# Group statistics of a normalisation: from averaging matmuls to transfers and VectorE sums

## Chip, cores, metric

The kernel runs on one core of one Trainium2 chip. The metric is the time of one execution in microseconds (us), lower is better. Several executions were timed for every kernel; all that are compared here ran fast, at a granted TensorE clock that averages 0.99 to 1.00 of full speed over the execution.

## The reference, cut to what matters

The input is 8 images of 64 channels and 64x64 pixels. Two layers follow each other, both with an attention over the 4096 pixels of an image. Only layer 1 normalises by groups of channels:

```python
# layer 0: attention with 8-channel keys and queries, plus its input
x = _L0_conv_ref(x, Wf, bf, Wg, bg, Wh, bh)

# layer 1: 8 groups of 8 channels
xg  = x.reshape(b, 8, 8, h, w)
mu  = mean(xg, axis=(2, 3, 4))
var = mean((xg - mu) ** 2, axis=(2, 3, 4))
xn  = (xg - mu) * rsqrt(var + 1e-5) * gamma + beta
q, k, v = split(w_qkv @ xn)                  # 64 channels each
x = w_proj @ (softmax(q k^T / 8) v) + x
```

## The kernel before

The 128 partitions hold the 64 channels twice, one half of the image in each. VectorE collects per-channel moments while layer 0 writes its result. Layer 1 of image b then needs, on each partition, the mean and the variance of the channel's group, which is spread over 16 partitions, 8 in each half. The kernel before fetched them across partitions with two matmuls against an averaging matrix, each of one column:

```python
gavg = const.tile([P, 2, GROUPS, GS], F32, name="gavg")     # 1/16 within a group, else 0
nc.gpsimd.memset(gavg, 0.5 / GS)
# ... eight affine_select on GpSimd cut it to blocks ...

def channels():
    vector.bn_aggr(mv, self.st())                 # mean and variance of each row

def means():
    ps = pair()                                   # borrows two PSUM banks
    matmul(ps[:, 0, 0:1], gavg, mv[:, 0:1], start=True, stop=True)
    nc.scalar.copy(mu, ps[:, 0, 0:1])
    vector.tensor_sub(d, mv[:, 0:1], mu)
    vector.scalar_tensor_tensor(v, d, d, mv[:, 1:2], op0=ALU.mult, op1=ALU.add)

def deviations():
    ps = pair()
    matmul(ps[:, 0, 0:1], gavg, v, start=True, stop=True)
    nc.scalar.copy(ve, ps[:, 0, 0:1])
    vector.tensor_scalar_add(ve, ve, EPS)
    # ... 1/sqrt(ve) by four Newton steps on VectorE, times gamma ...

at = [18, 22, 26] if self.b == 0 else [16, 20, 24]
units = [(at[0], channels, False), (at[1], means, True), (at[2], deviations, True)]
# ... then, from step 27 (b == 0) or 26 on: normal(c), project(c), values(c)
```

The numbers in `at` are steps of the attention that runs meanwhile. One step is one block of scores, their exponentials on ScalarE, their sum on VectorE, and the weighted sum of an earlier block on TensorE. `True` means that the unit borrows a pair of the eight PSUM banks. In a layer-0 stage TensorE makes scores in groups that fill the free banks, so a loan makes one group smaller and shifts all later groups. The order of TensorE's matmuls is fixed in the program; VectorE's is fixed too until the first layer-1 stage begins.

## Time and profile before

| | before |
|---|---|
| time, median of 3 | 3051.95 us (3050.56 to 3053.05) |
| span of the profiled run | 3050.3 us |
| layer 0 of images 0 and 1 (here "the opening") | up to 335.93 us |
| first layer-1 stage | 335.93 to 566.91, 230.98 us |
| each other layer-1 stage but the last two | 230.98 or 230.99 us |
| each layer-0 stage between them | 144.64 to 144.67 us |

### The profile page before, as it was taken

How to read it: one execution, taken by the hardware profiler on the slowest of the kernel's cores; microseconds unless marked ns; L12 is line 12 of the kernel's file. 1: busy time of each engine (PE TensorE's matmuls, PEld its weight loads, DVE VectorE, ACT ScalarE, POOL GpSimd, SP SyncE). 2: the span in 40 equal slices, each digit the busy share in tenths (PEclk: the TensorE clock that was granted, in tenths of full speed). 3: DMA queues.
4: the chain of work that ended last, by engine and by line, in shares of the span. 5: the costliest groups of instructions: out<-in, count | busy, mean ns of one | idle time of the engine just before them, and what ended most of it. 6: DMA issues, size and time to landing. Idle time of an engine off the chain costs nothing.

```text
span 3050.3 us, 58859 instructions
## 1 busy us (share of the span) xinstructions
PE 3023.2 (99%) x25857; PEld 1287.4 (42%) x25857; DVE 2596.0 (85%) x1668; ACT 2036.3 (67%) x1972; POOL 16.7 (1%) x45
## 2 busy tenths in 40 slices
PE   8999999999999999999999999999999999999998
PEld 3333335433354333533345333453334533345555
DVE  6999987899778998789987899779997799877776
ACT  6878655786557865578655785558855588555554
POOL 2000000000000000000000000000000000000000
PEclk9999999999999999999999999999999999999999
DMA  3000010100101001010010100100001000000000
GB/s 79 22 8 11 19 40 16 32 1 15 40 19 29 1 15 40 22 25 1 16 40 23 25 1 15 43 22 22 1 22 40 19 8 1 16 22 16 9 15 13
DMA packets 69816, 62.89 MB, mean 21 GB/s; under 512 B 43104, under 2 KB 43152, under 8 KB 69552
## 3 DMA queue, kind: packets, MB, share of 16 engines
q1 hardware_dynamic: 68560, 58.90, 8.0%
q8 instruction: 204, 3.34, 0.5%
q14 instruction: 60, 0.49, 0.1%
q0 software_dynamic: 672, 0.12, 0.0%
q10 hardware_dynamic: 320, 0.04, 0.0%
HBM read 25.06 MB, written 8.65 MB: 11 GB/s over the span
## 4 chain that ended last, share of the span: by engine, by line
PE 95%; DVE 3%; issue 1%; ACT 1%; DMA 0%; SPq 0%; DVEq 0%; ACTq 0%
PE banks L150 95%; DVE esum_l L140 3%; ACT e_l L917 1%; DMA x<-in_x_dram 0%; ACT full_l L542 0%; DVE rt L140 0%; DVE w_l L140 0%; DVE x L140 0%; SPq L179 0%; DVE raw_l L140 0%; DVE st_l L140 0%; DVE raw_end L140 0%; DVE guess_l L140 0%; DVE xn_l L140 0%; DVEq L140 0%
## 5 line engine op out<-in xcount | busy, mean ns | idle before, releaser
L140 DVE TENSOR_TENSOR esum_l<-esum_l,e_l 128x2048 f32<-128x2048 f32 x895 | 2048.7, 2289 | 363.5 <-ACT e_l L876 313.5
L876 ACT ACTIVATE e_l<-banks 128x1024 f32<-128x1024 f32 x1024 | 992.7, 1021 | 782.8 <-PE banks L150 761.0
L150 PE MATMUL banks<-e_l,v_l 64*64 64x512 f32 (+2 forms) x8772 | 1118.2, 588 | 0.0
L917 ACT ACTIVATE e_l<-banks 128x512 f32<-128x512 f32 (+3 forms) x767 | 956.9, 1311 | 194.0 <-PE banks L150 178.1
L150 PE MATMUL banks<-kq_l 64*64 64x512 f32 (+1 forms) x8448 | 1028.3, 586 | 3.4 <-ACT e_l L917 3.2
L150 PE MATMUL banks<-e_l,vt_l 128*64 128x512 f32 (+1 forms) x4060 | 832.1, 550 | 0.0
L150 PEld LDWEIGHTS banks<-e_l,v_l 64*64 64x64 f32 (+1 forms) x8772 | 439.7, 134 | 505.0 <-issue 466.8
L150 PEld LDWEIGHTS banks<-kq_l 64*64 64x64 f32 (+1 forms) x8448 | 422.9, 135 | 503.8 <-issue 468.3
L150 PEld LDWEIGHTS banks<-e_l,vt_l 128*64 128x64 f32 x4060 | 267.1, 137 | 471.3 <-issue 451.2
L150 PE MATMUL banks<-fg_l 32*128 32x512 f32 x1792 | 210.8, 460 | 6.4 <-ACT e_l L917 4.1
L150 PEld LDWEIGHTS banks<-fg_l 32*128 32x128 f32 x1792 | 85.9, 183 | 189.9 <-ACT e_l L917 139.1
L140 DVE TENSOR_TENSOR esum_l<-e_l,e_l 128x2048 f32<-128x2048 f32 x64 | 146.4, 2287 | 7.1 <-ACT e_l L876 7.1
L140 DVE TENSOR_TENSOR esum_l<-esum_l 128x1024 f32<-128x1024 f32 x63 | 76.9, 1221 | 0.9
L140 DVE TRANSPOSE_TENSOR_REDUCE part_l<-esum_l 128x32 f32<-128x1024 f32 x32 | 63.1, 1973 | 0.0
L140 DVE COPY raw_l<-banks 128x512 f32<-128x512 f32 x31 | 21.4, 692 | 30.6 <-PE banks L150 30.6
L140 DVE TENSOR_TENSOR raw_l<-raw_l,r_l 128x512 f32<-128x512 f32 x63 | 43.2, 685 | 0.0
L669 ACT ACTIVATE kq_l<-banks,qkb 128x512 f32<-128x512 f32 x64 | 40.6, 696 | 0.0
L150 PE MATMUL banks<-xn_l,wqk 64*64 64x512 f32 x256 | 35.5, 592 | 0.0
L150 PEld LDWEIGHTS banks<-wh,x 64*64 64x64 f32 x1024 | 25.3, 139 | 13.3 <-issue 12.4
L150 PEld LDWEIGHTS banks<-wvp,xn_l 64*64 64x64 f32 x1024 | 24.0, 134 | 13.0 <-issue 13.0
L577 ACT COPY raw_l<-banks 128x512 f32<-128x512 f32 x32 | 19.1, 596 | 11.6 <-PE banks L150 11.4
L140 DVE SCALAR_TENSOR_TENSOR x<-raw_l,hb,x 128x512 f32<-128x512 f32 x32 | 24.1, 752 | 1.1
(111 smaller groups left out, 404.4 us busy)
## 6 DMA issues: line engine op xcount, KB each, us to landing
r_l<-recips SPq DMA_DIRECT2D x126, 128.0 KB, 2.9
fg_l<-high_l SPq DMA_DIRECT2D x216, 64.0 KB, 2.0
kq_l<-kq_l SPq DMA_DIRECT2D x64, 128.0 KB, 2.3
out_dram<-raw_l SPq DMA_DIRECT2D x62, 128.0 KB, 2.4
x<-in_x_dram SPq DMA_DIRECT2D x30, 256.0 KB, 4.9
kq_l<-high_l SPq DMA_DIRECT2D x32, 64.0 KB, 2.0
part_l<-part_l SPq DMA_DIRECT2D x128, 4.0 KB, 1.8
zt_l<-zs_l SPq DMA_DIRECT2D x124, 1.0 KB, 1.7
```

The costliest lines, as they stand in the source:

```text
L140: it = getattr(nc.vector, name)(*args, **kwargs)
L150: in_order(nc.tensor.matmul(*args, **kwargs))
L577: nc.scalar.copy(raw, acc[0])
L669: nc.scalar.activation(self.parts[:, h, cols], ps[:, h, :], AF.Identity, bias=k1["qkb"][:, h : h + 1],)
L876: nc.scalar.activation(e[:, p], both_ps[p], AF.Exp, scale=at.scale)
L917: nc.scalar.activation(e.rearrange("k p h n -> k (p h) n")[:, first_ : first_ + n_, :], banks[:, bank : bank + n_, :], AF.Exp, scale=at.scale,
```

## The change

The intent: no matmul for the statistics. The mean and variance of each of the 128 rows (128x2 numbers, both halves of the image) go out to memory in one transfer and come back in four, laid out so that each partition has the 16 values of its group in its own row. VectorE sums them there. The units that read them are tied behind a sum of the steps before, so that the scheduler does not place them before the transfers have landed. The diff, with the removal of the averaging matrix and the move of a helper cut:

```diff
+    moments = [dram.tile([P, 2], F32, name=f"moments_{b}") for b in range(B)]
...
             def channels():
                 vector.bn_aggr(mv, self.st())
+                sent = moments[self.b]
+                nc.sync.dma_start(sent, mv)
+                for s in range(2):
+                    rows = sent[ts(s, C), :].rearrange("(g k) i -> g (k i)", k=GS)
+                    for h in range(2):
+                        nc.sync.dma_start(
+                            group[ts(h, C), s, :, :],
+                            rows.unsqueeze(1).broadcast_to([GROUPS, GS, 2 * GS]),
+                        )

             def means():
-                ps = pair()
-                matmul(ps[:, 0, 0:1], gavg, mv[:, 0:1], start=True, stop=True)
-                nc.scalar.copy(mu, ps[:, 0, 0:1])
-                vector.tensor_sub(d, mv[:, 0:1], mu)
-                vector.scalar_tensor_tensor(v, d, d, mv[:, 1:2], op0=ALU.mult, op1=ALU.add)
+                vector.tensor_reduce(mu, mean, axis=AX.X, op=ALU.add)
+                vector.tensor_scalar(mu, mu, 0.5 / GS, None, op0=ALU.mult)
+                vector.tensor_scalar(d, mean, mu, None, op0=ALU.subtract)
+                vector.tensor_mul(d, d, d)
+                vector.tensor_add(d, d, var)
+                vector.tensor_reduce(ve, d, axis=AX.X, op=ALU.add)

             def deviations():
-                ps = pair()
-                matmul(ps[:, 0, 0:1], gavg, v, start=True, stop=True)
-                nc.scalar.copy(ve, ps[:, 0, 0:1])
-                vector.tensor_scalar_add(ve, ve, EPS)
+                vector.tensor_scalar(ve, ve, 0.5 / GS, EPS, op0=ALU.mult, op1=ALU.add)
...
-            at = [18, 22, 26] if self.b == 0 else [16, 20, 24]
-            units = [(at[0], channels, False), (at[1], means, True), (at[2], deviations, True)]
+            at = [18, 23, 26] if self.b == 0 else [16, 22, 24]
+            units = [
+                (at[0], channels, False),
+                (at[1], behind(means), False),
+                (at[2], behind(deviations), False),
+            ]
```

`group` is a new tile of 128x32; `mean` and `var` are its two halves, and `d` becomes a tile of 16 columns.

More of the change, by code (lines that the diff above doesn't have):

```diff
@@ L122, in fast_path @@
     made_last = {}
+    added = None
     tight = False
@@ L150, in matmul, with behind, made @@
         in_order(nc.tensor.matmul(*args, **kwargs))
+    def behind(work_):
+        def made():
+            with tc.issue_after(added):
+                work_()
+        return made
     x_tiles = {}
@@ L229, in fast_path @@
     nc.vector.memset(ones, 1.0)
-    gavg = const.tile([P, 2, GROUPS, GS], F32, name="gavg")
-    nc.gpsimd.memset(gavg, 0.5 / GS)
-    for h in range(2):
-        for half in range(2):
-            rows = gavg[ts(half, C), h, :, :]
-            nc.gpsimd.affine_select(
-                out=rows, in_=rows, compare_op=ALU.is_ge, fill=0.0,
-                base=0, pattern=[[-GS, GROUPS], [0, GS]], channel_multiplier=1,
-            )
-            nc.gpsimd.affine_select(
-                out=rows, in_=rows, compare_op=ALU.is_ge, fill=0.0,
-                base=GS - 1, pattern=[[GS, GROUPS], [0, GS]], channel_multiplier=-1,
-            )
-    gavg = gavg.rearrange("p h g s -> p (h g s)")
     QP = 2 * CW // P
     stash = const.tile([P, (2 * B * NC - 1) * QP], F32, name="stash")
+    moments = [dram.tile([P, 2], F32, name=f"moments_{b}") for b in range(B)]
     recips = [dram.tile([P, QP], F32, name=f"recips_{i}") for i in range(2 * B * NC)]
@@ L597, in before @@
             mu = small.tile([P, 1], F32, tag="mu", name=f"mu_{n}")
-            v = small.tile([P, 1], F32, tag="v", name=f"v_{n}")
+            ve = small.tile([P, 1], F32, tag="ve", name=f"ve_{n}")
             self.mu, self.a = mu, small.tile([P, 1], F32, tag="a", name=f"a_{n}")
+            group = small.tile([P, 2, GS, 2], F32, tag="group", bufs=1, name=f"group_{n}")
+            mean, var = (group[:, :, :, i].rearrange("p s k -> p (s k)") for i in range(2))
+            d = small.tile([P, 2 * GS], F32, tag="d", bufs=1, name=f"d_{n}")
             def channels():
                 vector.bn_aggr(mv, self.st())
-            def means():
-                ps = pair()
-                matmul(ps[:, 0, 0:1], gavg, mv[:, 0:1], start=True, stop=True)
-                nc.scalar.copy(mu, ps[:, 0, 0:1])
-                d = small.tile([P, 1], F32, tag="d", name=f"d_{n}")
-                vector.tensor_sub(d, mv[:, 0:1], mu)
-                vector.scalar_tensor_tensor(v, d, d, mv[:, 1:2], op0=ALU.mult, op1=ALU.add)
-            def deviations():
-                ps = pair()
-                matmul(ps[:, 0, 0:1], gavg, v, start=True, stop=True)
-                ve = small.tile([P, 1], F32, tag="ve", name=f"ve_{n}")
-                nc.scalar.copy(ve, ps[:, 0, 0:1])
-                vector.tensor_scalar_add(ve, ve, EPS)
+                sent = moments[self.b]
[7 more added lines that the diff above has]
+                        )
+            def means():
+                vector.tensor_reduce(mu, mean, axis=AX.X, op=ALU.add)
[4 more added lines that the diff above has]
+                vector.tensor_reduce(ve, d, axis=AX.X, op=ALU.add)
+            def deviations():
+                vector.tensor_scalar(ve, ve, 0.5 / GS, EPS, op0=ALU.mult, op1=ALU.add)
                 guess = small.tile([P, 1], I32, tag="guess", name=f"guess_{n}")
@@ L753, in fast_path @@
     acc = esum = first = None
-    added = None
     def due_part(ready, room):
@@ L817, in finished @@
             steps = (now + delay + wait, now + delay + 2 * wait)
-        def behind(work_):
-            def made():
-                with tc.issue_after(added):
-                    work_()
-            return made
         at_step(steps[0], behind(reciprocals), 0)
```

## The prediction

> **What bounds the kernel now.** I read first the page's busy times, the row of the granted clock and the chain that ended last:
>
> ```profile
> PE 3023.2 (99%) x25857; PEld 1287.4 (42%) x25857; DVE 2596.0 (85%) x1668; ACT 2036.3 (67%) x1972; POOL 16.7 (1%) x45
> PEclk9999999999999999999999999999999999999999
> PE 95%; DVE 3%; issue 1%; ACT 1%; DMA 0%; SPq 0%; DVEq 0%; ACTq 0%
> ```
>
> TensorE is busy for 99% of 3050.3 us at the full clock, and 95% of the chain is its matmuls. A busy TensorE is not proof that nothing else paces it, so I then cut the span by stage. The kernel works through layer 0 of images 0 and 1 (to about 336 us), then alternates a layer-1 stage (231.6 us) with a layer-0 stage (144 us). The windows view, one row for each stretch (length, then busy time of TensorE, its weight loads, VectorE, ScalarE):
>
> ```profile
> 145.00:272.00 127.00, 121.41 (x727) 42.23 (x725) 121.55 (x82) 99.44 (x87) 0.00 (x0) 0.99 0.03 7
> 336.00:567.60 231.60, 231.60 (x2362) 105.43 (x2362) 184.72 (x141) 131.45 (x142) 0.00 (x0) 1.00 0.11 27
> 711.60:943.20 231.60, 231.60 (x2360) 105.22 (x2358) 187.34 (x142) 131.41 (x142) 0.00 (x0) 1.00 0.11 27
> ```
>
> In a layer-1 stage TensorE never stops, while VectorE has 231.60 - 184.72 = 46.9 us free. From 145 to 272 us it is another matter: the chain in order of time goes there through VectorE's sums of the exponentials, ScalarE waits for them, and TensorE has slack. So a microsecond of TensorE work is worth a microsecond in a layer-1 stage and next to nothing between 145 and 272 us; VectorE work is the reverse.
>
> Where does the changed code lie? The statistics of image b's layer 1 are placed by step: for image 0 near 227 to 246 us, in the VectorE-paced stretch; for images 1 to 7 inside the layer-1 stage of the image before, the TensorE-paced one. The build order of both kernels confirms this. The timeline of TensorE around one such pair of statistics (start, length, instructions):
>
> ```profile
> 405.82 1.04 PE L150 MATMUL banks<-e_l,v_l 64*64 64x512 f32 x8
> 406.68 1.90 PE L150 MATMUL banks<-kq_l 64*64 64x512 f32 x16
> 408.50 0.38 PE L150 MATMUL banks<-mv_l,gavg 128*128 128x1 f32 x2
> 408.81 1.95 PE L150 MATMUL banks<-e_l,v_l 64*64 64x512 f32 x16
> 410.58 1.90 PE L150 MATMUL banks<-kq_l 64*64 64x512 f32 x16
> 412.30 1.90 PE L150 MATMUL banks<-e_l,v_l 64*64 64x512 f32 x16
> 414.01 1.90 PE L150 MATMUL banks<-kq_l 64*64 64x512 f32 x16
> ...
> 420.88 1.90 PE L150 MATMUL banks<-kq_l 64*64 64x512 f32 x16
> 422.71 0.38 PE L150 MATMUL banks<-v_l,gavg 128*128 128x1 f32 x2
> 423.02 1.95 PE L150 MATMUL banks<-e_l,v_l 64*64 64x512 f32 x16
> 424.79 1.47 PE L150 MATMUL banks<-kq_l 64*64 64x512 f32 x12
> ```
>
> Read the starts, not the lengths, since the ends overlap. Two undisturbed blocks of 16 take 414.01 - 410.58 = 3.43 us. With a statistics matmul between them they take 410.58 - 406.68 = 3.90 us, and again 424.79 - 420.88 = 3.91 us. So one such matmul of a single column costs about 0.475 us of the bounding engine, more than the 0.31 us from its own start to the next one: the block before it lasts 1.82 instead of 1.716, the one after it 1.77.
>
> **What the Trainium skill says.** "TensorEngine Tiling (Array Packing)", Key Properties, says that changing the tiling mode drains TensorE. The attention here runs in 64x64 tiles and the statistics in 128x128, so each costs two changes; the trace agrees, with 0.10 us before and 0.05 us after beyond the 0.31 us itself. "TensorE: Matmul & The Clock Gate", The mechanism, says that matmuls are strictly in order, so one that waits for VectorE holds back all behind it; the trace shows it once, for image 0 (1.45 us idle before the matmul at 227.57 us, released by VectorE), and not in the layer-1 stages. "VectorE: DVE Perf Modes", on the TRN2 errata, gives each operation a fixed cost; the trace agrees: operations on a single column take 0.15 to 0.22 us. "DMA: Bandwidth & Descriptors", Anatomy of one DMA, gives about 2 us of fixed cost a transfer; the small ones here land in 1.4 us (reciprocals to memory) and 1.7 us (rows of sums).
>
> **The change, part by part.**
>
> Removed on TensorE: 16 such matmuls (each recorded as two passes). 14 lie in layer-1 stages: 14 x 0.475 = 6.7 us, all on the path. I checked the same difference at all seven pairs: 3.90 or 3.91 us each time, once 3.98. The two for image 0 lie where VectorE paces.
>
> Removed on ScalarE: 16 copies of 0.168 us, 2.7 us, not on the path in layer-1 stages (100 us free there).
>
> VectorE: removed are a subtraction (0.15) and a fused multiply-add (0.22) per image; added are two reductions, three elementwise operations on 16 columns and a scaling; the step that added the epsilon stays as one instruction. Nearest rows: a reduction of 32 elements to 8 takes 0.20 us, single-column operations 0.15 to 0.16. From start to start each costs some 0.19 us, so 6 x 0.19 - 0.45 = about 0.7 us more per image. For images 1 to 7 that sits in the 46.9 us free. For image 0 it is on the path, but a wait of VectorE goes with the matmul:
>
> ```profile
> 242.16 0.15 DVE L140 TENSOR_SCALAR ve_l<-ve_l 128x1 f32<-128x1 f32 x1 [0.62 <-ACT ve_l L617]
> ```
>
> The net there is 0.7 - 0.62, about +0.1 us. In addition the two matmuls of image 0 each borrowed a pair of PSUM banks from the scores, and the build order shows one group of scores fewer over the two opening stages (84 against 85). The TensorE-paced end of that stage, 272 to 336 us, might gain from the new grouping; I allow -0.5 us, give or take 1.5, an estimate.
>
> Added on the DMA queue: five small transfers per image, one out and four back. For image 0 I reckon: aggregation ends at 227.4, out 1.4 us later, four issues at 0.56 us, 1.7 us to land, so at about 233 us. In the new order VectorE first does four sums of 2.33 us, reaching the group means at about 236.8. Margin about 3.5 us. In the layer-1 stages six steps of 3.43 us lie between, 20 us, against some 6 us. The transfers are hidden.
>
> Removed on GpSimd: nine instructions that built the averaging matrix before 13 us. The first matmul waits for the input until 7.3 us, not for them. Nothing, or a few tenths either way, as the loads of layer 1's constants move forward by some 4 us.
>
> Sum: -6.7 + 0.1 - 0.5 = -7.1, so 3051.95 - 7.1 = 3045, a ratio of 1.002.
>
> **The rivals.**
>
> One: the transfers become the wait. For it: VectorE is in order, and a late transfer stops the sums that pace the opening. Against it: the margin of 3.5 us. If they came 5 us later than reckoned, one stall of 1.5 us in the opening, none later: 3047.
>
> Two: VectorE's extra work shows fully and regrouping the scores costs time. Dropping two loans also moves every later projection of image 0 to another place in the groups, and the last group before layer 1 becomes 7 banks instead of 5. ScalarE needs about 0.85 us longer for it, against 0.92 us free before the next scores in the old trace. With these the opening could lose 2 us: -6.7 + 2, 3047.
>
> Three: the matmul's gap is filled by something else. If the 0.475 us were partly a wait that stays (the following block waiting for its weights or for ScalarE), only the 0.31 us would return: 14 x 0.31 = 4.3 us, 3047.6. Against it: no wait of TensorE appears at these places, and undisturbed blocks keep 1.716 us.
>
> Four: the freed rotation of bank pairs changes the phase in which layer-1 and layer-0 stages meet (it came back to the same place at every stage, and now drifts by two thirds of a turn). For no effect: at the boundary at 711.58 us ScalarE has emptied the last bank 0.92 us before. If it did matter, it could cost up to 1 us at four boundaries: 3049.
>
> **Range and chances.** All rivals end above the sum, but only within 4 us; the good side is regrouping in the opening, 1 to 2 us more. Runs of the same kernel differ by 2.5 us. So 3042 to 3048.5 holds it 8 times in 10. Two per cent is 61 us; even the whole idle time of TensorE is 27 us, so a gain of that size is all but excluded (chance 0.005); a loss of that size needs a stall in every stage of which I see no sign (0.01). Within 2%: 0.985.
>
> **What would show it.** Right: no statistics matmul in the trace; the layer-1 stages 1 to 7 shorter by 0.95 us each, so the period of image to image 374.65 instead of 375.6; the blocks of 16 evenly 1.716 us apart; no wait of VectorE on the gathered group tile; the layer-0 stages unchanged at 144 us; the start of the first layer-1 stage within 2 us of 336. Wrong: a wait of VectorE for a transfer near 237 us; a period that shrank by less than 0.6 us; new waits of TensorE for ScalarE at the stage boundaries; or a layer-0 stage that grew.

## More of the kernel before

A stage is read off TensorE's timeline, from the first matmul of the stage's scores to that of the next.

The fence is VectorE's timeline of the kernel before; the columns are start, length, engine, line, operation, output<-inputs, shapes, count, and in brackets any idle time before with its releaser:

```profile
227.16 0.26 DVE L140 BATCH_NORM_AGGREGATE mv_l<-st_l 128x2 f32<-128x24 f32 x1
227.34 2.23 DVE L140 TENSOR_TENSOR esum_l<-e_l,e_l 128x2048 f32<-128x2048 f32 x1
229.67 2.29 DVE L140 TENSOR_TENSOR esum_l<-esum_l,e_l 128x2048 f32<-128x2048 f32 x1
231.88 0.15 DVE L140 TENSOR_TENSOR d_l<-mv_l,mu_l 128x1 f32<-128x1 f32 x1
232.07 0.22 DVE L140 SCALAR_TENSOR_TENSOR v_l<-d_l,mv_l 128x1 f32<-128x1 f32 x1
232.20 9.34 DVE L140 TENSOR_TENSOR esum_l<-esum_l,e_l 128x2048 f32<-128x2048 f32 x4
```

VectorE goes from sum to sum of the exponentials without a gap, 2.29 us each; the statistics are small steps between two of them. Here every microsecond that VectorE spends delays the next sum. The two small steps take 232.20 - 231.88 = 0.32 us from start to start.

## The result, and the profile after

| | before | changed |
|---|---|---|
| time, median of 4 runs of each on one chip | 3052.5 (3050.56 to 3053.83) | 3046.85 (3046.04 to 3047.8) |
| ratio, changed to before | | 0.9982, 95% interval 0.9965 to 0.9999 |
| span of the profiled run | 3050.3 | 3044.9 |
| start of the first layer-1 stage | 335.93 | 335.85 |
| first layer-1 stage | 230.98 | 230.90 |
| each other layer-1 stage but the last two | 230.98 | 230.04 |
| layer-0 stages | 144.64 to 144.67 | 144.64 to 144.66 |

A ratio is the mean time of one kernel's fast runs over the mean of the other's fast runs of the same rounds, so it is not quite the ratio of the medians. The changed kernel is 0.2% faster: within 2%, and 1.85 us above the 3045.0 predicted.

**Where the gain is.** TensorE's timeline of the changed kernel, around the place where the two statistics matmuls of image 1 stood:

```profile
404.02 1.90 PE L151 MATMUL banks<-kq_l 64*64 64x512 f32 x16
405.74 1.90 PE L151 MATMUL banks<-e_l,v_l 64*64 64x512 f32 x16
407.45 1.90 PE L151 MATMUL banks<-kq_l 64*64 64x512 f32 x16
409.17 1.90 PE L151 MATMUL banks<-e_l,v_l 64*64 64x512 f32 x16
```

All starts are 1.71 or 1.72 us apart. The matmul of one column is gone, and with it the lengthened blocks of 1.82 and 1.77 us beside it. The windows view of the changed kernel for the first and the second layer-1 stage, each row with its length and the busy time of TensorE, its weight loads, VectorE and ScalarE:

```profile
335.85:566.75 230.90, 230.90 (x2354) 105.15 (x2353) 185.02 (x145) 131.30 (x139) 0.00 (x0) 1.00 0.11 27
711.41:941.45 230.04, 230.04 (x2351) 104.87 (x2349) 186.63 (x146) 131.30 (x139) 0.00 (x0) 1.00 0.11 27
```

The second stage lost 230.98 - 230.04 = 0.94 us, two matmuls of 0.47. The first lost only 0.08. The reason stands at its start. TensorE in the kernel before:

```profile
335.93 1.95 PE L150 MATMUL banks<-kq_l 64*64 64x512 f32 x16
337.81 2.80 PE L150 MATMUL banks<-e_l,v_l 128*64 128x512 f32 x12
340.53 1.95 PE L150 MATMUL banks<-kq_l 64*64 64x512 f32 x16
```

and in the changed kernel:

```profile
335.85 1.95 PE L151 MATMUL banks<-kq_l 64*64 64x512 f32 x16
337.73 3.65 PE L151 MATMUL banks<-e_l,v_l 128*64 128x512 f32 x16
341.31 1.95 PE L151 MATMUL banks<-kq_l 64*64 64x512 f32 x16
```

The new grouping of the opening leaves 16 instead of 12 weighted-sum matmuls of layer 0 to be done after the first scores of layer 1. The block takes 341.31 - 337.73 = 3.58 us instead of 2.72, so 0.86 us of work have moved from the opening over the boundary. That is a lesson in reading stages: a boundary that is defined by one matmul moves when the order around it moves. From here on the opening and the first layer-1 stage are taken together.

**Where the gain was spent.** VectorE's timeline of the changed kernel at the statistics of image 0:

```profile
229.07 7.08 DVE L141 TENSOR_TENSOR esum_l<-esum_l,e_l 128x2048 f32<-128x2048 f32 x3
236.07 0.16 DVE L141 TENSOR_REDUCE mu_l<-group_l 128x1 f32<-128x16 f32 x1
...
237.15 0.17 DVE L141 TENSOR_REDUCE ve_l<-d_l 128x1 f32<-128x16 f32 x1
237.23 7.07 DVE L141 TENSOR_TENSOR esum_l<-esum_l,e_l 128x2048 f32<-128x2048 f32 x3
```

The six new steps take 237.23 - 236.07 = 1.16 us of the engine that paces this stretch, against 0.32 before, and no bracket stands at the first one: VectorE did not wait for the transfers. The chain of waits in order of time seems to say the opposite (start, length, what):

```profile
226.85 3.07 DMA moments<-mv_l
229.94 0.70 SPq L610
...
231.97 1.97 DMA group_l<-moments
...
234.02 2.05 issue
```

The chain walks back from the reduction to the semaphore that it needed, and so through the transfers. But the row "issue 2.05" says that the data was there at 234.02 and the reduction began at 236.07; the sums of the fence before fill that time. A chain names the last release that it finds, not the work in between. So the transfers were hidden, with 2.05 us to spare.

**The account**, from the traces of the two kernels. The last TensorE instruction ends 5.95 us earlier: the opening gives 0.08 (its scores happened to start 0.59 us earlier, so it was in fact longer by 0.5), the first layer-1 stage 0.08, five stages 0.94 each, 4.7 together, and the last two stages with the end 1.02; rounding and the layer-0 stages hold the rest. From there to the end of the span the changed kernel takes 0.55 us longer, so 5.4 remain. This last part stays open: apart from a cast of 0.15 us on ScalarE, nothing but the output's transfer is recorded in it. It ranged from 7.0 to 7.75 us in the kernels with the new statistics for image 0, and from 6.6 to 6.8 in the three traces of kernels with the matmuls there.

### The profile page after: what moved, and what is told of

It reads as the page before. It is cut to its first block, busy times and chain, and to the rows that moved or that the text cites. A ratio compares the mean times of both kernels' runs of the same rounds, so it can differ in the third digit from the quotient of the medians.

```text
span 3044.9 us, 58882 instructions
## 1 busy us (share of the span) xinstructions
PE 3014.8 (99%) x25833; PEld 1301.2 (43%) x25833; DVE 2598.9 (85%) x1700; ACT 2035.5 (67%) x1955; POOL 13.3 (0%) x36
## 4 chain that ended last, share of the span: by engine, by line
PE 95%; DVE 3%; issue 1%; ACT 1%; DMA 0%; SPq 0%; DVEq 0%; ACTq 0%
PE banks L151 95%; DVE esum_l L141 2%; ACT e_l L920 1%; DMA x<-in_x_dram 0%; DMA moments<-mv_l 0%; ACT full_l L539 0%; DMA group_l<-moments 0%; SPq L610 0%; DVE rt L141 0%; DVE w_l L141 0%; DVE x L141 0%; SPq L189 0%; DVE st_l L141 0%; DVE raw_l L141 0%; DVE raw_end L141 0%
## 5 line engine op out<-in xcount | busy, mean ns | idle before, releaser
L920 ACT ACTIVATE e_l<-banks 128x1536 f32<-128x1536 f32 (+3 forms) x766 | 956.7, 1312 | 196.2 <-PE banks L151 178.7
L151 PEld LDWEIGHTS banks<-e_l,v_l 64*64 64x64 f32 (+1 forms) x8780 | 450.3, 133 | 505.7 <-issue 462.3
L151 PEld LDWEIGHTS banks<-kq_l 64*64 64x64 f32 (+1 forms) x8448 | 431.2, 135 | 496.6 <-issue 460.4
```

Source lines behind the costliest of these rows:

```text
L151: in_order(nc.tensor.matmul(*args, **kwargs))
L920: nc.scalar.activation(e.rearrange("k p h n -> k (p h) n")[:, first_ : first_ + n_, :], banks[:, bank : bank + n_, :], AF.Exp, scale=at.scale,
```

## The experiments

Twelve kernels ran; each was timed against the kernel before on the same chip. Kernels are compared only within the same rounds. All gave correct results. The "fourth group of scores" is TensorE's block of scores that starts near 27 to 28 us; counting from it takes out the start, which differs from run to run (27.23 to 28.24 us).

Two questions were put. In the layer-1 stages: is it the matmul's own time that returned, and what is it made of? In the opening: what ate some 0.5 to 1.3 us? For the second there were four theories: a stall of TensorE behind ScalarE, seen in the trace after; the new grouping of the scores without the loans of banks; VectorE's longer statistics; and TensorE work that lies before a VectorE-paced limit and so is free in one order and not in the other.

| kernel | median us (range) | ratio to before (95%) | opening + first layer-1 stage, excess us |
|---|---|---|---|
| before, first | 3052.08 (3050.65 to 3053.6) | 1 | -0.07 (first trace) and -0.02 (before_again) |
| after_again | 3046.49 (3046.28 to 3047.75) | 0.9982 (0.9968 to 0.9996) | 0.66; the first trace had 1.31 |
| dev_25 | 3046.07 (3045.29 to 3046.81) | 0.9980 (0.9966 to 0.9993) | 0.84 |
| img0_by_matmul | 3044.71 (3044.48 to 3045.46) | 0.9976 (0.9963 to 0.9990) | 0 |
| img0_only | 3053.21 (3052.83 to 3054.7) | 1.0005 (0.9991 to 1.0018) | 1.21 |
| before, second | 3052.09 (3051.39 to 3054.2) | 1 | |
| proj_30 | 3045.94 (3045.56 to 3046.69) | 0.9978 (0.9964 to 0.9991) | 0.51 |
| dev_24 | 3049.67 (3049.16 to 3050.77) | 0.9991 (0.9976 to 1.0006) | 3.3 |
| extra_128 | 3053.03 (3052.72 to 3054.14) | 1.0002 (0.9987 to 1.0017) | 0.64 |
| extra_64 | 3047.95 (3047.61 to 3048.14) | 0.9984 (0.9969 to 0.9999) | 0.64 |
| before, third | 3051.71 (3050.49 to 3054.0) | 1 | |
| loan_kept | 3046.26 (3045.85 to 3047.06) | 0.9983 (0.9969 to 0.9996) | 0.71 |
| loan_gpsimd | 3048.52 (3048.22 to 3049.19) | 0.9990 (0.9976 to 1.0004) | 2.1 |
| loan_29 | 3046.65 (3046.45 to 3048.16) | 0.9985 (0.9971 to 0.9999) | 0.92 |

The last column is read from the traces: the time from the fourth group of scores to the layer-0 stage after the first layer-1 stage, less what the one-column matmuls inside it cost (0.95 us for two of 128x128, 0.23 for two sets of 64x64), less the 537.97 us of img0_by_matmul. The kernel before has 537.90 and 537.95 so reckoned in its two traces. Those two and img0_by_matmul lie within 0.07 us, but the changed program repeats only within 0.65, so differences below that between kernels with the new statistics are not read, unless what follows accounts for them.

**What the scatter goes with.** The granted TensorE clock is not constant within the opening. The windows view in steps of 1 us shows it at 0.50 of full speed for some 7 us or more between 15 and 26 us in every trace, and once more, for about 3.4 us (6.8 in extra_128), in every trace but that of loan_kept. This second time comes early (within 225 to 236 us) in both traces of the kernel before, in img0_by_matmul, after_again, extra_128, extra_64, loan_29 and loan_gpsimd, and late (within 248 to 257 us) in the first trace of the changed kernel, img0_only, dev_25, proj_30 and dev_24. The windows view from 253 to 256 us, first of the first trace of the changed kernel, then of after_again; the figure after the last bracket is the granted clock:

```profile
253.00:256.00 3.00, 3.00 (x12) 0.79 (x12) 2.90 (x2) 2.54 (x3) 0.00 (x0) 0.52 0.00 0
253.00:256.00 3.00, 3.00 (x19) 1.02 (x18) 2.79 (x2) 2.45 (x3) 0.00 (x0) 1.00 0.00 0
```

The same 20 matmuls, from the first projection of image 0 to the next scores, took 258.19 - 252.72 = 5.47 us in the first trace and 257.06 - 253.06 = 4.00 us in after_again. Of these 1.47 us, 0.65 are left when the first layer-1 stage starts. Five traces have this program for image 0: the three with the early low clock have an excess of 0.66, 0.64 and 0.64, the two with the late one 1.31 and 1.21 (img0_only). So the scatter goes with where the low clock falls: some 0.65 us of excess without it, some 0.6 more with it. What decides where it falls is not shown, and no run was made to test it.

### after_again: the changed kernel once more

No edit. It is the control.

> The changed kernel again, as a control for what varies from execution to execution. In its first trace the opening was 0.6 us ahead of the old kernel at 27.5 us. Theory A (chance: the first input arrived 0.1 us earlier and TensorE's clock rose a little sooner): the lead at that point may be anything from 0 to 0.7 us here. Theory B (GpSimd no longer builds the averaging matrix, so the opening really is faster): 0.6 us again, the start of the fourth group of scores at 27.5 us. Either way: VectorE reaches the group means without a wait, TensorE stalls near 252 us for about 2.2 us, layer-1 stages 230.9 us (first) and 230.04 us (the others). Total 3046 to 3048.

Measured: ratio 0.9982 once more. Its trace speaks against the first theory about the opening. TensorE's timeline of the first trace of the changed kernel:

```profile
252.29 0.50 PE L151 MATMUL banks<-kq_l 32*128 32x512 f32 x3 [2.21 <-ACT e_l L920]
```

and of after_again:

```profile
252.63 0.50 PE L151 MATMUL banks<-kq_l 32*128 32x512 f32 x3 [1.57 <-ACT e_l L920]
```

A stall of 2.21 us behind ScalarE, which itself waited 3.01 us for VectorE's sums, looked like the loss. The same program then stalled 1.57 us at the same place, and its opening was 0.65 us shorter. The difference goes with the clock, as shown above.

### dev_25: the statistics' second half one step earlier

```diff
-            at = [18, 23, 26] if self.b == 0 else [16, 22, 24]
+            at = [18, 23, 25] if self.b == 0 else [16, 22, 24]
```

> The changed kernel with the second part of image 0's statistics one step earlier (25 for 26). TensorE's order is exactly that of the changed kernel; VectorE's differs only in that two sums now stand between the small operations and the first normalisation, which were back to back. Theory A (the opening lost about 1.4 us because 3.8 us of small VectorE work in one piece kept ScalarE waiting 3.0 us and so TensorE 2.2 us): the wait of ScalarE falls to under 1.5 us, that of TensorE to under 1 us, the first layer-1 stage starts 1.0 to 1.5 us earlier (near 334.6), total 3045.5. Theory B (the opening lost it by the new grouping of scores over banks, whatever VectorE does): stall and start unchanged within 0.3 us, total 3046.8.

Measured: the stall of 2.21 us became two of 0.67 and 1.04, and the first layer-1 stage started 307.91 us after the fourth group, no sooner than in after_again (307.73) and 0.47 us sooner than in the first trace, where the stall theory had asked for 1.0 to 1.5. The time is that of after_again within the runs' scatter. The stall theory is not supported: the stall was split and the opening hardly moved. The low clock fell late here too (249 to 253 us).

### img0_by_matmul: image 0 by matmul, images 1 to 7 by transfers

```diff
+            by_matmul = self.b == 0
...
+            if by_matmul:
+                at = [18, 22, 26] if self.b == 0 else [16, 20, 24]
+                units = [
+                    (at[0], channels, False),
+                    (at[1], means_old, True),
+                    (at[2], deviations_old, True),
+                ]
```

`means_old` and `deviations_old` are those of the kernel before, with the averaging matrix; some small tiles have one buffer instead of two, because the on-chip memory did not hold both versions.

> Images 1 to 7 by transfers and VectorE as in the change, image 0 by the two matmuls as before. Theory A (each removed matmul in a layer-1 stage returns 0.475 us, and the opening lost some): opening as in the old kernel, first layer-1 stage starts near 335.9 and lasts 230.98 - 0.95 = 230.03 us, all others 230.04, total 6.6 us below the old kernel, so 3045.9 and about 0.9 below the changed one. Theory B (the opening gained by the change, as GpSimd has less to do): total above the changed kernel by 0.1 to 0.6.

Measured: 3044.71 us, 1.8 below after_again, and the ranges do not overlap. It is the fastest kernel. Of the 1.8 us, by the two traces, 0.66 lie in the opening, 0.29 in the chance start, and 0.83 in the unexplained time after the last TensorE instruction. The windows view of its first layer-1 stage:

```profile
335.41:565.45 230.04, 230.04 (x2352) 104.15 (x2350) 184.49 (x145) 131.30 (x139) 0.00 (x0) 1.00 0.11 27
```

The stage has the full gain, and the opening is as long as in the kernel before (307.93 us from the fourth group, before 307.87 and 307.91). It has the averaging matrix built on GpSimd, and its fourth group starts at 27.48 us, no later than that of the changed kernel without the matrix (27.47 and 27.77): the nine instructions were not on the path.

### img0_only: the reverse

```diff
+            by_matmul = self.b > 0
```

> The reverse: only image 0 by transfers and VectorE, images 1 to 7 by matmuls as before. Theory A: TensorE's stall near 252 us is there; the first layer-1 stage lasts 231.8 us (230.98 and 0.86 us of four weighted sums moved into it from the opening), the others 230.98; total equal to the old kernel or up to 1 us above it. Theory B (the removal of image 0's matmuls is worth what each of the others is): total 0.95 us below the old kernel.

Measured: 3053.21 us, not faster than before. The second and later layer-1 stages take 230.98 us as in the kernel before. With img0_by_matmul it splits the change into two: all the gain comes from images 1 to 7, and the transfers for image 0 gave none. Its excess of 1.21 us is among the larger ones; its low clock fell late, at 252 to 257 us.

### extra_128 and extra_64: what a one-column matmul costs, and why

Both add two dummy matmuls of constants at the old places for images 1 to 7. Nothing waits for them and they wait for nothing but their turn and a free pair of banks. The first has the old shape, the second covers the same 128x128 in four matmuls of 64x64, the tile shape of the matmuls around.

```diff
+            def extra():                                     # extra_128
+                ps = pair()
+                matmul(ps[:, 0, 0:1], ident, ident[:, 0:1], start=True, stop=True)
...
+            def extra():                                     # extra_64
+                ps = pair()
+                for m in range(2):
+                    for h in range(2):
+                        matmul(
+                            ps[ts(m, C), h, 0:1], ident[ts(h, C), 0:C], ident[ts(h, C), 0:1],
+                            start=True, stop=True,
+                        )
...
+            if self.b > 0:                                   # both
+                units += [(20, extra, True), (24, extra, True)]
```

> The changed kernel with two matmuls added in each layer-1 stage that had lost two: same shape as the removed ones (128x128 weights, one column), same steps, but from constants, waiting for nothing, and nobody reads the result. Theory A (the cost is the matmul and the change of tiles): 0.475 us each, layer-1 stages 230.98 again (the first 231.85), total 6.7 us above the changed kernel. Theory B (a part of it was the dependence on VectorE and on ScalarE's copy): 0.31 us each, stages 230.66, total 4.3 us above.

> The same addition, but as four matmuls of one column in 64x64 tiles at the positions that the attention uses, so that the tile shape never changes. Theory A (what costs is the change of tile shape, twice for each): at most 0.2 us for each set of four, stages at most 230.45, total at most 2.8 us above the changed kernel. Theory B (what costs is a short matmul as such, whatever its tile): 0.4 us or more for each set, stages 230.85 or more.

TensorE's timeline of extra_128 around the dummy:

```profile
406.81 1.90 PE L151 MATMUL banks<-kq_l 64*64 64x512 f32 x16
408.64 0.38 PE L151 MATMUL banks<-ident 128*128 128x1 f32 x2
408.95 1.95 PE L151 MATMUL banks<-e_l,v_l 64*64 64x512 f32 x16
```

and of extra_64:

```profile
406.84 1.90 PE L151 MATMUL banks<-kq_l 64*64 64x512 f32 x16
408.56 0.24 PE L151 MATMUL banks<-ident 64*64 64x1 f32 x8
408.64 1.93 PE L151 MATMUL banks<-e_l,v_l 64*64 64x512 f32 x16
```

Measured: extra_128 restores the layer-1 stage of 230.98 us to the hundredth, and the time of before (ratio 1.0002). So the cost was the matmul's own, not a wait for its data or its reader; that it lies in the loan of the banks is excluded by extra_64, which borrows the same. In extra_64 the stage is 230.27, so each set of four costs (230.27 - 230.04) / 2 = 0.115 us, although it makes eight passes where the other makes two. The block before lasts 1.72 us from start to start there, as undisturbed, and 1.83 in extra_128. The remaining 0.47 - 0.115, about 0.36 us, is what the 128x128 shape costs between blocks of 64x64. It was not split further. The weight loads are a part of it: those of extra_128 begin at 408.64 us, with the matmul, after the block before has ended, while the first of extra_64 begin at 408.13, inside that block; so a weight load that is no longer hidden and the change of shape itself cannot be told apart here. A matmul of one column is cheap in the shape of its neighbours.

### dev_24: the transfers given less time

```diff
-            at = [18, 23, 26] if self.b == 0 else [16, 22, 24]
+            at = [18, 22, 24] if self.b == 0 else [16, 22, 24]
```

> The changed kernel with image 0's statistics at steps 22 and 24 for 23 and 26, so that VectorE reaches the group means after two sums instead of four. The gathered tile landed at about 234.0 us in the trace of the change; VectorE would be there at about 231.5. Both theories: a wait of VectorE for the transfers of 2 to 2.7 us. Theory C or D (the opening is paced by VectorE there): it shows nearly in full, first layer-1 stage 1.5 to 2.5 us later, total 3048 to 3049. Rival (TensorE's buffers of scores absorb it): start unchanged within 0.4 us.

VectorE's timeline of dev_24:

```profile
229.45 2.29 DVE L141 TENSOR_TENSOR esum_l<-esum_l,e_l 128x2048 f32<-128x2048 f32 x1
234.61 0.17 DVE L141 TENSOR_REDUCE mu_l<-group_l 128x1 f32<-128x16 f32 x1 [2.87 <-DMA group_l<-moments]
```

Measured: with two sums fewer ahead of it, the reduction now waits 2.87 us for the transfers, VectorE needs 23.61 us from the aggregation to the first normalisation instead of 20.4 in the kernel before (3.2 more), and the excess is 3.3 us. This is the first rival of the prediction, made on purpose. In this run a microsecond of VectorE in this stretch was about a microsecond of the kernel (its low clock fell late, so a part of the 3.3 may be that). With one sum fewer the change would have had little or no margin left: loan_kept below shows it.

### proj_30: the normalised input one step earlier

```diff
-            at = [18, 23, 26] if self.b == 0 else [16, 22, 24]
+            at = [18, 23, 25] if self.b == 0 else [16, 22, 24]
...
-                s = 31 + 8 * c if self.b == 0 else 30 + 8 * c
+                s = 30 + 8 * c if self.b == 0 else 30 + 8 * c
```

> The changed kernel with image 0's projections one step earlier (steps 30, 38, 46, 54 for 31, 39, 47, 55), and so their normalisations too; second part of the statistics at step 25. The build order shows the first projection one group of scores earlier and one group of scores fewer in the opening (the last one still 7 banks). Theory C (new, since the stall near 252 us proved harmless: up to about 255 us VectorE's sums pace the opening, through the six buffers of exponentials, so TensorE work before that point is free; the wider groups pushed the first projection, 1.0 to 1.4 us, behind it): the first layer-1 stage starts about 1 us earlier relative to the fourth group of scores (306.9 for 307.9 us), total 3045.3. Theory D (the opening is as long as VectorE's work to its end, so the order of TensorE's work is indifferent): 307.7 to 308.4 us as in all kernels so far, total 3046.5.

Measured: ratio 0.9978, excess 0.51. That is 0.3 us better than dev_25, less than the same program's two traces differ. The theory of free TensorE work is not supported.

### loan_kept: the old grouping with the new statistics

```diff
+            if self.b == 0:
+                units += [(22, lambda: None, True), (26, lambda: None, True)]
```

Two units that do nothing borrow the banks at the old steps, so the scores fall into the same groups as in the kernel before. One more thing differs: three sums instead of four now stand before the group means.

> The changed kernel, but for image 0 the two loans of a pair of PSUM banks are kept at steps 22 and 26, with nothing done in them. TensorE's order is then that of the old kernel without the two matmuls (same groups of scores, last group of 5, four weighted sums not deferred); VectorE works as in the change. Theory B (the regrouping of the scores lost it: the changed opening is as long as the old one although 0.86 us of its work went to the layer-1 stage): opening 307.6 to 308.2 us from the fourth group of scores to the first layer-1 stage, and that stage 230.04 instead of 230.90, total 3045.5, 0.9 below the changed kernel. Rival E (VectorE's added work, 0.57 us net by the traces, lost it): opening 308.4 to 308.8, stage 230.04, total within 0.4 of the changed kernel.

Measured: the first layer-1 stage is 230.04 us, so the four matmuls are back in the opening, and the opening is 0.73 to 0.77 us longer than before. The reduction waited 0.33 us for the transfers, and VectorE's interval from the aggregation to the first normalisation is 21.07 us instead of 20.40. No low clock falls near the statistics. The sum and the time are those of the changed kernel (0.9983). With the old groups the loss is still there, so the grouping did not make it; the new grouping moves work over the boundary and costs nothing that can be read.

### loan_gpsimd: the Newton steps on GpSimd

```diff
+                on = nc.gpsimd if self.b == 0 else vector
-                vector.tensor_scalar(
+                on.tensor_scalar(
                     guess, guess, -1.0, float(0x5F3759DF), op0=ALU.mult, op1=ALU.add
                 )
...
-                    vector.scalar_tensor_tensor(w, y, y, ve, op0=ALU.mult, op1=ALU.mult)
-                    vector.tensor_scalar(w, w, -0.5, 1.5, op0=ALU.mult, op1=ALU.add)
-                    vector.tensor_mul(y, y, w)
+                    on.tensor_mul(w, y, y)
+                    on.tensor_mul(w, w, ve)
+                    on.tensor_scalar(w, w, -0.5, 1.5, op0=ALU.mult, op1=ALU.add)
+                    on.tensor_mul(y, y, w)
...
```

It has the empty loans as well, and the second half at step 23. If VectorE paces, some 3 us taken from it should shorten the opening.

> The same with image 0's Newton steps (some 18 small operations, about 3 us of VectorE) on GpSimd, which is idle, and the second part of the statistics at step 23. Theory F (VectorE's sums pace the opening to about 255 us): sums some 3 us ahead at 248 us, opening shorter by 1 to 2 us, total 3044. Theory G (TensorE's groups pace it just as much): VectorE gains idle time, opening shorter by less than 0.5 us, total 3045.5 as without it. If GpSimd is slower than the four steps allow (9.6 us), VectorE waits for it before the first normalisation and the opening gets longer.

GpSimd's timeline of loan_gpsimd:

```profile
243.15 2.31 POOL L640 TENSOR_SCALAR w_l<-w_l 128x1 f32<-128x1 f32 x1
245.55 0.19 POOL L641 TENSOR_TENSOR guess_l<-guess_l,w_l 128x1 f32<-128x1 f32 x1
```

and VectorE's:

```profile
235.94 9.47 DVE L141 TENSOR_TENSOR esum_l<-esum_l,e_l 128x2048 f32<-128x2048 f32 x4
249.33 0.55 DVE L141 TENSOR_SCALAR xn_l<-x,mu_l,a_l 128x512 f32<-128x512 f32 x1 [3.92 <-POOL a_l L642]
```

Measured: slower than loan_kept by 2.3 us. Beside VectorE's sums a GpSimd step on one column took 2.15 to 2.32 us, as long as a sum (2.29); once VectorE had run out of sums, 0.19. VectorE then waited 3.92 us for the result. The Trainium skill, "SBUF — State Buffer", section "SBUF: two separate sides", says that VectorE and GpSimd share a pair of ports as "an exclusive lock, not a bandwidth split", which a VectorE operation with two inputs in SBUF holds for its whole length against a GpSimd operation that reads SBUF. The sums are such operations, and the trace agrees. As a way to relieve VectorE it failed; as a test of the pace it counts: VectorE's interval is 1.6 us longer than in the kernel before, and the excess 2.1.

### loan_29: loan_kept with earlier projections

```diff
-            at = [18, 23, 26] if self.b == 0 else [16, 22, 24]
+            at = [18, 23, 24] if self.b == 0 else [16, 22, 24]
...
-                s = 31 + 8 * c if self.b == 0 else 30 + 8 * c
+                s = 29 + 8 * c if self.b == 0 else 30 + 8 * c
```

plus the two empty loans.

> As the first of this call, with image 0's projections two steps earlier (29, 37, 45, 53) and the second part of the statistics at step 24. The first projection comes one group of scores earlier, the second too, at about 268 us, where the old trace still showed ScalarE waiting for VectorE. Theory C (TensorE work is free only while VectorE paces): opening 0.5 to 1.2 us shorter than with the projections at 31. Rival G: within 0.4 us of it, as moving them by one step did little.

Measured: excess 0.92 against 0.71 of loan_kept, no gain. The theory of free TensorE work predicted a gain twice, here and in proj_30, and got none that stands out of the scatter.

### before_again: the kernel before, one look

No edit; a second trace of the kernel before.

> The old kernel again, for a second trace of its opening: fourth group of scores somewhere between 27.2 and 28.1 us, first layer-1 stage 307.6 to 308.1 us later and 230.98 us long, layer-0 stages 144.65. If the opening were as short as 307.2, the change would have lengthened it by more than I now hold.

Measured: 3051.5 us in a single run. The opening takes 307.91 us from the fourth group against 307.87 in the first trace, and the fourth group starts at 27.47 instead of 28.06. So the 0.59 us by which the changed kernel started earlier were chance.

## Why the prediction was right, point by point

**The 6.7 us of TensorE time: right.** Stages shrank by 0.94 us, and extra_128 gives the same cost for a matmul that nobody waits for. The third rival, that only 0.31 us of each would return, is refuted. The working from differences of starts was what carried this; the recorded lengths would have given less. (Its lengths of 231.6 and 144 us for the two kinds of stage are those of its windows; the stages are 230.98 and 144.65, with the same period.) What the prediction did not know is how the 0.475 splits: about 0.36 goes with the 128x128 shape, 0.115 is the cost of the same work in 64x64.

**The opening: the sign of a term was wrong.** Predicted was -0.4 us, made of +0.1 for VectorE and -0.5 for the grouping. Measured for opening and first layer-1 stage together is +0.5 to +1.3 in the kernels that did not delay VectorE on purpose: near 0.65 with the program of the change, and 1.2 to 1.3 where the low clock fell late. Two terms failed. The regrouping gave nothing: loan_kept, with the old groups, takes as long as the changed kernel. The term had been a guess in the direction of hope, with 1.5 either way. And VectorE's net was not 0.1 but 0.55 us: the interval from aggregation to first normalisation grew from 20.40 to 20.95 us. The added steps cost 1.16 - 0.32 = 0.84 instead of 0.7: the six new ones were sized right (6 x 0.19 = 1.14), the two removed ones were counted with 0.45 where the starts show 0.32. The wait of 0.62 did go, and about 0.3 more came on top: the seven sums between the two points take 9.33 + 6.99 = 16.32 us instead of 4.54 + 9.34 + 2.21 = 16.09, and the steps after them 3.30 instead of 3.19. A likely reason is that in the kernel before a small step more often began before the sum in front had ended, and a sum before the step in front; that was read from the timelines and not tested. The late low clock, which added some 0.6 us in two traces, was in no term.

**Rival two was the nearest.** It said that VectorE's work shows fully and regrouping costs time, up to 2 us. The first half is supported by three kernels that delayed VectorE by other amounts: 3.2 us more on VectorE gave 3.3 (dev_24), 1.6 gave 2.1 (loan_gpsimd), and 0.67 gave 0.7 (loan_kept, this one within the scatter). The second half is not supported. Not settled is the remainder: dev_25 and proj_30 have only 0.25 us more on VectorE than before and an excess of 0.84 and 0.51. The low clock fell late in both, which may be the rest of it; that was not tested.

**The transfers are hidden: right, with less to spare than reckoned.** The margin is 2.05 us, not 3.5 (the prediction's own 236.8 - 233 would be 3.8). The outgoing transfer held up the first gather for 3.1 us (226.85 to 229.94) instead of 1.4; the row that gave 1.4 us was for another transfer. VectorE arrived 9.5 us after the start of the aggregation, close to the 9.6 reckoned. dev_24 shows that two sums earlier it would have failed.

**Phase of the bank pairs: no effect, as thought.** The layer-0 stages lie within 144.63 to 144.68 us in every kernel. **GpSimd's nine instructions: no effect, as thought**, shown by img0_by_matmul.

**The sum.** In place of -6.7 + 0.1 - 0.5 it is -6.7 + 0.7 for opening and grouping together, and some +0.5 in the unexplained ending, so about -5.5; the timed medians differ by 5.65. The unexplained ending was in no term, and neither was the clock. The range held because the rivals had been counted on its upper side.

## What to carry to other kernels

A tiny operation on the bounding engine costs what it does to its neighbours: take the difference of starts of the blocks around it, with and without, and look whether it forces another tile shape. The same edit can pay in one stage and cost in another when different engines pace them, so apply it by stage; here the mixed kernel beats both. When a boundary moves, compare the sum of the stages on both sides, and look at a second trace of the same program, with the granted clock in short windows beside it, before a single stall becomes a theory.

## What the Trainium skill lacked or had wrong

- "TensorEngine Tiling (Array Packing)", Key Properties, says that changing the tiling mode drains TensorE but gives no cost. Here about 0.36 us went with the 128x128 shape between 64x64 blocks, weight loads that were no longer hidden included: a one-column matmul of 128x128 between 64x64 blocks cost 0.47 us, four one-column matmuls of 64x64 in the same place 0.115 us.
- "DMA: Bandwidth & Descriptors" has no figure for a round trip of small transfers through memory that SyncE issues, one out and four back. Here it took 7.2 us (226.85 to 234.02): 3.07 us until the outgoing transfer was done and the first gather could be issued, and 1.97 us from the last gather's start to its landing.
- "SBUF — State Buffer" is right on the shared ports, and lacks a number for a small GpSimd step beside two-input VectorE work: 2.15 to 2.32 us instead of 0.19.
- No page explains why the time from the last TensorE instruction to the end of the span differs between kernels with the same ending, from 6.6 to 7.75 us; it stays unexplained.
